# A macaron transformer block on one Trainium2 core: Winograd's seven block products in the global attention's value projection, and every local product on quarters of the array

## The chip, the cores and the metric

The kernel runs on one core of one Trainium2 chip; all data are fp32. The metric is device time in microseconds (us) of one execution; lower is better. Times of the kernel before are the median of three runs. Profiles are of one further execution each, with the granted TensorE clock beside the span (0.995 of full speed here).

## The reference

For 8 batches of 512 tokens with 256 channels, three stages follow one another:

```python
x = x + 0.5 * ffn(layernorm(x))        # two layers of local attention + GLU
x = x + global_attention(layernorm(x)) # 16 heads
x = x + 0.5 * ffn(layernorm(x))        # the same two layers, same weights

def global_attention(y, weight):
    heads = y.reshape(b, t, 16, 16).transpose(0, 2, 1, 3)
    attn = softmax(heads @ heads^T / 4)              # 512 x 512 for each head
    o = attn @ y                                     # every head averages whole rows of y
    return concat(o) @ weight                        # weight: (16*256, 256)

def local_attention(q, k, v):   # 8 heads of 64, windows of 128 tokens
    # a query sees its own window up to itself, and the window before from (i - 128) on
    return softmax(8 * q @ k^T + mask) @ v
```

Each ffn layer shifts half of the channels by a token, projects to q, k, v (`wqkv`), normalises and rotates q and k, runs the local attention, projects by `wo`, and then runs a GLU of width 682.

## The kernel before

**Who does what.** Two streams (`stream`, keys k = 0 and 1) run the ffn blocks, each for four batches, twice over; a third (`global_stream`) runs the global attention of a batch as soon as its first ffn is done. The three are interleaved step by step (each `yield` is a step). Nothing is issued directly: every operation is recorded with a rank, and `Plan.order` (line 270) then sets one static order for each engine by list scheduling, with a cost for each operation (`Plan.cost`, line 233), ring buffers for tiles, and a charge when TensorE changes the shape in which its array is used (`MODE`, line 183, names "whole", "columns", "halves", "quarters", "fours"). On the chip each engine's queue, SP's DMA queue too, runs in that order and waits at semaphores. All instructions carry the line of the planner's issuing loop (L369), so groups are told apart by tile names.

**TensorE.** An fp32 matmul appears as two MATMUL records, each with a weight load (LDWEIGHTS) of its own; counts below are of records. Tile names: `psum_bank` is any of the 8 PSUM banks.

**Global attention** (`global_heads`, line 956). For a batch: layernorm, then `zT`, the transposed activations as two tiles of 128 channels by 512 tokens (`work_gz`, lines 963 to 970). Since `attn @ y @ W_h = attn @ (y @ W_h)`, each head h first projects all tokens: y (512 x 256) times its block W_h (256 x 256). `front(h)` (line 975) loads W_h (`work_wa`, two buffers) and the head's 16 channels (`work_hT`, four small DMAs, two buffers) and gives three steps: `scores()` (line 987; four score tiles in four banks, Exp by ScalarE into `work_e`) and `project(0)`, `project(1)` (line 998). One `project` makes two token tiles of 128: four matmuls with 128 x 128 stationary operands from `zT` and 256 moving columns of W_h, then one VectorE copy of a whole bank into `work_xw`. So a head has 8 matmuls, 16 records. `attend(head, t)` (line 1017) multiplies: four matmuls of 256 columns, then one VectorE instruction that scales by 1/sum and adds to x. The loop at line 1031 runs the steps of head h+1 among the four `attend` of head h.

**Local attention** (`attention`, line 566). For each token tile t: `front(t)` (q, k, v), `scores(t)` (line 630), `values(t)` (line 732), `project(t)` (line 797, by `wo`). GpSimd (POOL) computes the rotary half `work_t`, the -0.5 power `small_rn` and the scaling of the probabilities. `far` is true for the middle six of each stream's eight blocks: there transposes go through DRAM and, for t > 0, both products run on 64 x 64 quarters of the array and leave out key halves that the mask removes. For the first tile (`nk == 1`), and for all tiles of the first and last block ("near"), scores use 64 rows by 128 columns ("halves", line 657) and values use 128 rows by 64 columns ("columns", lines 761 to 773), with one ScalarE copy `work_o<-psum_bank` after.

**GLU** (`glu`, line 819). The last 43 hidden rows of two token tiles are multiplied side by side in the two halves of the array (line 919).

**Weights.** `wo` of both layers stays resident (`load_attention`, line 393), GLU weights are loaded anew for each step by the second stream.

Of the kernel before, what the change touches and what calls it, by code (L numbers as in the profile page):

```python
# [11 lines left out]
ALU = mybir.AluOpType  # L12
# [164 lines left out]
class Plan:  # L177
# [55 lines left out]
    def cost(self, op):  # L233

        if op.engine == "tensor":

            lanes, op.mode = {}, "whole"
            for name, args, kw in op.calls:
                lane, t = 0, 109.0
                if name == "matmul":  # L240
                    a = kw["lhsT"]
                    lane, t = (a.region()[0], args[0].region()[0]), 2 * max(0.842 * elements(kw["rhs"]), 0.852 * a.shape[1])
                    k, m = a.shape
                    op.mode = "fours" if k <= 32 else "quarters" if k == m == 64 else "halves" if k <= 64 else "columns" if m <= 64 else "whole"
                lanes[lane] = lanes.get(lane, 0.0) + t
            busy = max(lanes.values())
            return busy, busy + 170
        name, args, kw = op.calls[0]
        n = max(elements(a) for a in (*args, *kw.values()) if hasattr(a, "shape"))
        if name == "dma_start":  # L250
            return 580.0, 2300.0
        if op.engine == "scalar":
            if name == "activation":
                op.mode = {AF.Exp: "exp", AF.Gelu: "gelu"}.get(args[2])
                busy = 70 + 0.82 * n + (105 if "bias" in kw else 0)
                return (busy + 93, busy + 310) if "accum_out" in kw else (busy, busy + 110)
            return 70 + 0.81 * n, 175 + 0.81 * n
        if op.engine == "vector":
            if name == "tensor_tensor_reduce":
                return 90.0 + n, 250.0 + n  # L260
            if name == "bn_stats":
                return 70.0 + n, 150.0 + n
            return 90 + 1.035 * n, 170 + 1.035 * n
        if name == "memset":
            return 80 + 0.85 * n, 100 + 0.85 * n
        if ALU.pow in args:
            return 350.0 + 157 * n, 400.0 + 157 * n
        return 210 + 1.98 * n, 250 + 1.98 * n
# [107 lines left out]
def macaron(ctx: ExitStack, tc: tile.TileContext, x, weight, wqkv, wo, w1, w2, b2, vecs, qk_scales, rotary, out):  # L376
# [16 lines left out]
    def load_attention(l):  # L393

        wq = wpool.tile([P, 2, 3 * INNER], F32, tag=f"wqkv{l}", name=f"wqkv{l}")
        for part in range(3):
            cols = slice(part * INNER, (part + 1) * INNER)
            nc.sync.dma_start(out=wq[:, :, cols], in_=wqkv[l, :, cols].rearrange("(k p) f -> p k f", p=P))
        o = wpool.tile([P, NPAIR, D], F32, tag=f"wo{l}", name=f"wo{l}")
        nc.sync.dma_start(out=o, in_=wo[l].rearrange("(k p) f -> p k f", p=P))  # L400
        return wq, o

    def load_glu(l):

# [18 lines left out]
    load_x(0)  # L423
    load_x(1)
    attention_weights = [load_attention(0)]
    glu_weights = [load_glu(0)]
    attention_weights.append(load_attention(1))
    tabs, vec = [], []
# [134 lines left out]
            later_of[k] = d.rearrange("p w -> (p w)").rearrange("(n f) -> n f", f=P)  # L563
        return later_of[k]

    def attention(k, y, l, far):
        wqkv_sb, wo_sb = attention_weights[l]
        z0 = zpool.tile([P, N + 1], F32, tag=f"z{k}", bufs=2)
        tiled = lambda t, c: y[:, t, c * P : (c + 1) * P]
        nc.scalar.copy(z0[:, :N], transposed(tiled, 0))  # L570
# [59 lines left out]
        def scores(t, pair, rn):  # L630
# [21 lines left out]
            for g in range(2):  # L652
# [1 line left out]
                quarters = far and nk == 2  # L654
                sps = [bank([P, 2, 3 * HALF if quarters else nk * P]) for _ in range(2)]

                pieces = [(slice(0, P), slice(0, nk * P), slice(0, nk * P))]
                if quarters:

                    pieces = []  # L660
# [71 lines left out]
        def values(t, probs):  # L732

            nk = min(t, 1) + 1
            o = work.tile([P, NPAIR, P], F32, tag="o", bufs=2)
            if far and nk == 2:

                pos = [bank([P, NPAIR, P]) for _ in range(2)]
                for g in range(2):
                    with plan.together():  # L740
                        for i in range(2):
                            for n in range(2):
                                for half in range(2):

                                    j = (1 - half, half)[n]
                                    q = slice(half * 2, half * 2 + 2) if n else slice(0, 4)
                                    rows = slice(half * HALF, (half + 1) * HALF)
                                    for par in range(2):
                                        h = 2 * i + par
                                        hd = 4 * g + h  # L750
                                        nc.tensor.matmul(
                                            pos[half][par * DH : (par + 1) * DH, 2 * g + i, q.start * 32 : q.stop * 32],
                                            lhsT=v[t - 1 + j][rows, hd * DH : (hd + 1) * DH],
                                            rhs=probs[g][rows, j, q, h, :],
                                            start=(n == 0),
                                            stop=(n == 1),
                                        )
                nc.scalar.copy(o, pos[0])
                nc.vector.tensor_add(o, pos[1], o)
                return o  # L760
            po = bank([P, NPAIR, P])

            def products(pair, turned):
                for j in range(nk):
                    for par in range(2):
                        hd = 2 * pair + par
                        nc.tensor.matmul(
                            po[par * DH : (par + 1) * DH, pair, :],
                            lhsT=v[t - (t + j) % 2][:, hd * DH : (hd + 1) * DH],
                            rhs=turned(par, j),  # L770
                            start=(j == 0),
                            stop=(j == nk - 1),
                        )

            if far:
                for g in range(2):
                    with plan.together():
                        for i in range(2):
                            products(2 * g + i, lambda par, j: probs[g][:, j, :, 2 * i + par, :])
            else:  # L780
                turned = []
                for n in range(NPAIR + 2):
# [7 lines left out]
                        turned.append(pT)  # L790
                    if n >= 2:
                        with plan.together():
                            products(n - 2, lambda par, j: turned[n - 2][:, par, j, :])
            nc.scalar.copy(o, po)
            return o

        def project(t, oT):
# [9 lines left out]
        for t in range(NT):  # L807
# [7 lines left out]
            o = values(t, probs)  # L815
            yield
        project(NT - 1, o)

    def glu(k, y, step, xb, far):
        l = step % DEPTH  # L820
# [90 lines left out]
        for t in (0, 2, 1, 3):  # L911
# [7 lines left out]
            with plan.together():  # L919
                for at, q in ((0, t - 2), (TAIL, t)):  # L920
                    rows = slice(at, at + LAST + 1)
                    nc.tensor.matmul(
                        pys[q],
                        lhsT=us[FULL][rows, q * P : (q + 1) * P],
                        rhs=w2_sb[rows, FULL, :],
                        start=False,
                        stop=True,
                    )
            for q in (t - 2, t):
                nc.vector.tensor_add(y[:, q, :], pys[q], y[:, q, :])  # L930
                if l == DEPTH - 1:
# [3 lines left out]
    def stream(k, blocks):  # L935

        for n, (b, second) in enumerate(blocks):
# [4 lines left out]
            for l in range(DEPTH):  # L942
                step = DEPTH * n + l
                far = FAR and 0 < n < len(blocks) - 1
                yield from attention(k, y, l, far)
                yield from glu(k, y, step, xs[b], far)

                if k == 1 and step + 1 < DEPTH * len(blocks):
# [7 lines left out]
    def global_heads(b):  # L956
# [13 lines left out]
            zT.append(z)  # L970

        def front(h):

            w = work.tile([P, 2, D], F32, tag="wa", bufs=2)
            nc.sync.dma_start(out=w, in_=weight[h * D : (h + 1) * D, :].rearrange("(c p) f -> p c f", p=P))

            hT = work.tile([P, N], F32, tag="hT", bufs=2)  # L980
            at = h % (P // AHD) * AHD
            for i in range(4):
                nc.sync.dma_start(out=hT[32 * i : 32 * i + AHD, :], in_=zT[h * AHD // P][at : at + AHD, :])
            rsum = gsmall.tile([P, NT], F32, tag="rsum")
            es, xw = [], []

            def scores():
                sps = [bank([P, N]) for s in range(NT)]
# [4 lines left out]
                for s in range(NT):  # L993
                    e = work.tile([P, N], F32, tag="e", bufs=2 * NT)
                    nc.scalar.activation(e, sps[s], AF.Exp, scale=1.0 / AHD**0.5, accum_out=rsum[:, s : s + 1])
                    es.append(e)

            def project(half):
                pv = bank([P, 2, D])
                with plan.together():  # L1000
                    for i in range(2):
                        s = 2 * half + i
                        for c in range(2):
                            nc.tensor.matmul(
                                pv[:, i, :],
                                lhsT=zT[c][:, s * P : (s + 1) * P],
                                rhs=w[:, c, :],
                                start=(c == 0),
                                stop=(c == 1),
                            )  # L1010
                xv = work.tile([P, 2, D], F32, tag="xw", bufs=4)
                nc.vector.tensor_copy(xv, pv)
                xw.append(xv)

            return es, xw, rsum, (scores, lambda: project(0), lambda: project(1))

        def attend(head, t):
            es, xw, rinv, _ = head
            pa = bank([P, D])
            with plan.together():  # L1020
                for s in range(NT):
                    nc.tensor.matmul(
                        pa, lhsT=es[s][:, t * P : (t + 1) * P], rhs=xw[s // 2][:, s % 2, :], start=(s == 0), stop=(s == NT - 1)
                    )
            xt = xs[b][:, t, :]
            nc.vector.scalar_tensor_tensor(xt, pa, rinv[:, t : t + 1], xt, ALU.mult, ALU.add)
# [122 lines left out]
```

## Time and profile before

| | |
|---|---|
| median of 3 runs | 3955.65 us (3954.25 to 3959.32) |
| profiled execution | 3959.6 us, its span 3957.8 us |
| TensorE clock granted | 0.995 |
| DMA | 400 MB, mean 101 GB/s; HBM 96 GB/s |
| projection `psum_bank<-work_wa,work_gz` | 2048 records of 256 columns, 477.4 us busy |
| attend `psum_bank<-work_xw,work_e` | 4096 records of 256 columns, 959.5 us busy |

How to read it: busy time is the union of an engine's instruction durations. A MATMUL record's duration contains its way through the array, so neighbours overlap: its mean ("384 ns") is not its price. The price in a stream is the distance from start to start, which a timeline gives: a merged entry `start, length, x16` is followed by the next entry's start. "Idle before" is the time that an engine stood still ahead of a group and what released it.

### The profile page before, as it was taken

The page shows a single profiled execution, that of the slowest core. Times are in us where ns is not written, and L with a number is a line of the kernel's source. Part 1 is how long each engine was busy: PE and PEld are TensorE (multiplying, and loading weights), DVE is VectorE, ACT ScalarE, POOL GpSimd, SP SyncE. Part 2 cuts the span into 40 slices and gives each one's busy share as a digit, 9 for nine tenths or more (in the row PEclk, how much of TensorE's full clock was granted, in tenths as well). Part 3 has the DMA queues.
Part 4 walks back from the last instruction along what each step waited for, and adds up shares of the span by engine and source line. Part 5 has one row for each costly group of instructions (what it writes and reads, how often), then busy time and mean ns, then how long its engine had stood idle before and what let it go on. Part 6 is the DMA issues. An engine that isn't in the chain of part 4 may idle for free.

```text
span 3957.8 us, 67863 instructions
## 1 busy us (share of the span) xinstructions
PE 3892.5 (98%) x23808; PEld 2675.0 (68%) x23808; DVE 2422.4 (61%) x6832; ACT 1779.5 (45%) x4556; POOL 1226.6 (31%) x1132
## 2 busy tenths in 40 slices
PE   8999999999999999999999999999999999999998
PEld 5565776766767667676676766767677666677665
DVE  7575655666566665665765667566556665526573
ACT  5564434535344353453544545354345353324462
POOL 6242323434133241331523424143223231103240
PEclk9999999999999999999999999999999999999999
DMA  3000543534435244352443534435325344110000
GB/s 116 1 23 28 153 137 103 154 98 138 124 119 148 87 142 119 118 153 86 138 142 101 156 93 143 137 102 161 96 90 154 93 132 128 57 37 5 1 23 11
DMA packets 437625, 400.43 MB, mean 101 GB/s; under 512 B 53954, under 2 KB 379172, under 8 KB 437284
## 3 DMA queue, kind: packets, MB, share of 16 engines
q1 hardware_dynamic: 436420, 394.76, 33.7%
q8 instruction: 189, 3.10, 0.3%
q10 hardware_dynamic: 864, 1.33, 0.1%
q14 instruction: 152, 1.25, 0.1%
HBM read 235.49 MB, written 143.66 MB: 96 GB/s over the span
## 4 chain that ended last, share of the span: by engine, by line
PE 55%; DVE 3%; ACT 2%; issue 2%; POOL 1%; DMA 0%; SPq 0%; POOLq 0%; DVEq 0%; ACTq 0%
PE psum_bank L369 55%; ACT work_p L369 1%; DVE work_p L369 1%; DVE work_qn L369 1%; POOL small_rn L369 0%; DVE small_ss L369 0%; POOL work_t L369 0%; SPq L369 0%; ACT work_qn L369 0%; DVE xpool_x L369 0%; DMA work_both<-dram_turned 0%; DMA work_p<-dram_turned 0%; ACT work_sq L369 0%; DVE work_both L369 0%; ACT work_both L369 0%
## 5 line engine op out<-in xcount | busy, mean ns | idle before, releaser
L369 PE MATMUL psum_bank<-work_xw,work_e 128*128 128x256 f32 x4096 | 959.5, 384 | 3.6 <-ACT work_e L369 2.5
L369 PEld LDWEIGHTS psum_bank<-work_xw,work_e 128*128 128x128 f32 x4096 | 762.6, 190 | 203.4 <-issue 42.3
L369 PE MATMUL psum_bank<-wpool_wqkv,zpool_z 128*128 128x512 f32 x1536 | 703.6, 597 | 1.3 <-ACT work_o L369 1.3
L369 ACT ACTIVATE work_p<-work_p,small_nmax,small_rn 128x192 f32<-128x192 f32 (+2 forms) x1024 | 543.8, 533 | 288.9 <-DVE small_nmax L369 187.0
L369 POOL TENSOR_TENSOR work_t<-work_qn,const_tab 128x256 f32<-128x256 f32 x512 | 388.7, 780 | 713.3 <-ACT work_qn L369 691.7
L369 PE MATMUL psum_bank<-zpool_z,wpool_w 128*128 128x512 f32 x1280 | 560.9, 597 | 1.5 <-DVE zpool_z L369 1.2
L369 POOL TENSOR_TENSOR work_p<-work_p,small_ri 128x768 f32<-128x768 f32 (+1 forms) x192 | 267.6, 1395 | 871.2 <-DVE small_ri L369 410.0
L369 POOL TENSOR_TENSOR small_rn<-small_ss,const_nhalf 128x8 f32<-128x8 f32 x256 | 486.7, 1902 | 137.8 <-DVE small_ss L369 130.9
L369 PE MATMUL psum_bank<-work_wa,work_gz 128*128 128x256 f32 x2048 | 477.4, 381 | 3.0 <-DVE work_gz L369 2.8
L369 ACT ACTIVATE work_e<-psum_bank 128x512 f32<-128x512 f32 x512 | 298.7, 596 | 396.6 <-PE psum_bank L369 390.1
L369 PEld LDWEIGHTS psum_bank<-wpool_wqkv,zpool_z 128*128 128x128 f32 x1536 | 284.4, 191 | 276.6 <-issue 261.6
L369 PEld LDWEIGHTS psum_bank<-zpool_z,wpool_w 128*128 128x128 f32 x1280 | 244.2, 192 | 302.2 <-issue 279.8
L369 PEld LDWEIGHTS psum_bank<-work_wa,work_gz 128*128 128x128 f32 x2048 | 384.9, 190 | 73.2 <-issue 14.9
L369 DVE SCALAR_TENSOR_TENSOR xpool_x<-psum_bank,gsmall_rinv,xpool_x 128x256 f32<-128x256 f32 x512 | 242.9, 476 | 275.0 <-PE psum_bank L369 272.2
L369 ACT COPY work_qn<-psum_bank 128x512 f32<-128x512 f32 x256 | 148.5, 583 | 374.8 <-PE psum_bank L369 322.9
L369 DVE TENSOR_REDUCE small_ss<-work_sq 128x8 f32<-128x512 f32 x256 | 172.5, 674 | 133.7 <-ACT work_sq L369 133.1
L369 DVE SCALAR_TENSOR_TENSOR work_p<-psum_bank,const_vec,work_p 128x512 f32<-128x512 f32 x128 | 95.8, 749 | 252.6 <-PE psum_bank L369 203.4
L369 PE MATMUL psum_bank<-wpool_wo,work_o 128*128 128x256 f32 x1024 | 246.7, 384 | 2.5 <-DVE work_o L369 1.6
L369 DVE COPY work_xw<-psum_bank 128x512 f32<-128x512 f32 x256 | 174.2, 681 | 121.8 <-PE psum_bank L369 120.5
L369 PE MATMUL psum_bank<-wpool_w,work_p 128*128 128x256 f32 x1024 | 242.7, 380 | 0.0
L369 DVE TENSOR_TENSOR ypool_y<-psum_bank,ypool_y 128x256 f32<-128x256 f32 x256 | 101.7, 419 | 216.2 <-PE psum_bank L369 213.2
L369 ACT COPY work_o<-psum_bank 128x512 f32<-128x512 f32 x128 | 74.7, 583 | 340.8 <-PE psum_bank L369 335.7
(89 smaller groups left out, 5025.8 us busy)
## 6 DMA issues: line engine op xcount, KB each, us to landing
work_p<-dram_quarters SPq DMA_DIRECT2D x576, 128.0 KB
dram_quarters<-work_p SPq DMA_DIRECT2D x288, 192.0 KB
dram_turned<-work_both SPq DMA_DIRECT2D x96, 512.0 KB
work_both<-dram_turned SPq DMA_DIRECT2D x384, 128.0 KB
work_wa<-in_weight_dram SPq DMA_DIRECT2D x128, 256.0 KB
wpool_w<-in_w_dram SPq DMA_DIRECT2D x48, 640.0 KB
work_hT<-work_gz SPq DMA_DIRECT2D x512, 32.0 KB
dram_turned<-work_p SPq DMA_DIRECT2D x48, 256.0 KB
```

The source lines that it names most:

```text
L369: getattr(getattr(nc, op.engine), name)(*map(real, args), **{k: real(a) for k, a in kw.items()})
```

## The change

**1. Projection by Winograd's form of Strassen.** y is cut in blocks of 256 tokens by 128 channels (`a11 a12 / a21 a22`), W_h in blocks of 128 x 128 (`b11 b12 / b21 b22`). Seven block products take the place of eight; each is two matmuls with 128 x 128 stationary operands and 128 moving columns: 14 matmuls, 28 records for each head. The sums of y are made once for each batch, those of W_h for each head, all on POOL; the sums of the products on VectorE, with one ScalarE copy.

```diff
+        sums = work.tile([P, 4, N // 2], F32, tag="sums")
+        for i, (u, v, op) in enumerate(
+            ((a21, a22, ALU.add), (sums[:, 0], a11, ALU.subtract), (a11, a21, ALU.subtract), (a12, sums[:, 1], ALU.subtract))
+        ):
+            nc.gpsimd.tensor_tensor(sums[:, i], u, v, op)
...
-            w = work.tile([P, 2, D], F32, tag="wa", bufs=2)
+            w = work.tile([P, 2, 4, P], F32, tag="wa", bufs=2)
+            nc.gpsimd.tensor_tensor(diffs[:, :2], blocks[:, 1::2], blocks[:, :2], ALU.subtract)
+            t1, t3, t2, t4 = (diffs[:, i] for i in range(4))
+            nc.gpsimd.tensor_tensor(t2, b22, t1, ALU.subtract)
+            nc.gpsimd.tensor_tensor(t4, b21, t2, ALU.subtract)
-            hT = work.tile([P, N], F32, tag="hT", bufs=2)
+            hT = work.tile([P, N], F32, tag="hT", bufs=1)
+            xw = work.tile([P, 4, 2, P], F32, tag="xw", bufs=2)
...
+            def product(*pairs):
+                ps = bank([P, len(pairs), 2, P])
+                with plan.together():
+                    for i, (left, right) in enumerate(pairs):
+                        for t in range(2):
+                            nc.tensor.matmul(ps[:, i, t, :], lhsT=left[:, t * P : (t + 1) * P], rhs=right, start=True, stop=True)
...
             def project(half):
-                xv = work.tile([P, 2, D], F32, tag="xw", bufs=4)
-                nc.vector.tensor_copy(xv, pv)
+                if half == 0:
+                    p1 = product((a11, b11))
+                    u1 = work.tile([P, N // 2], F32, tag="u1")
+                    nc.scalar.copy(u1, p1[:, 0])
+                    nc.vector.tensor_add(pairs[:, 0], product((a12, b21), (s2, t2)), spread(u1))
+                    return
+                ps = product((s3, t3), (s1, t1))
+                nc.vector.tensor_add(pairs[:, 1], ps, spread(whole[:, 2]))
+                nc.vector.tensor_add(whole[:, 2], ps[:, 1], whole[:, 1])
+                nc.vector.tensor_add(pairs[:, 1], product((a22, t4), (s4, b22)), pairs[:, 1])
```

`attend` reads the same 256 columns as two pieces of 128 (`rhs=xw[:, (slice(0, 4, 3), slice(1, 3))[s // 2], s % 2, :]`).

**2. Local products on quarters everywhere.** Scores of the first tile and of near blocks are cut into two halves of the queries. `values` has one form for all: key halves go to two banks `pos[0]`, `pos[1]`, the part that the mask removes is left out, and after the ScalarE copy VectorE adds the second bank (all queries, or the later half for `nk == 1`). The GLU's last matmul is cut in two halves of 64 tokens. The planner names every matmul of at most 64 x 64 "quarters".

```diff
-                pieces = [(slice(0, P), slice(0, nk * P), slice(0, nk * P))]
+                pieces = [(slice(q, q + HALF), slice(0, nk * P), slice(0, nk * P)) for q in (0, HALF)]
...
-            nc.scalar.copy(o, po)
+            nc.scalar.copy(o, pos[0])
+            q = slice(HALF if nk == 1 else 0, P)
+            nc.vector.tensor_add(o[:, :, q], pos[1][:, :, q], o[:, :, q])
...
+                    for half in (0, HALF):
                         nc.tensor.matmul(
-                            pys[q],
-                            lhsT=us[FULL][rows, q * P : (q + 1) * P],
+                            pys[q][half : half + HALF, :],
+                            lhsT=us[FULL][rows, q * P + half : q * P + half + HALF],
```

**3. `wo` in one buffer.** It is loaded for layer 0 at the start and then, by the second stream at the end of its attention, for the next step: 15 further loads of 512 KB.

```diff
+    def load_wo(l):
+        o = wpool.tile([P, NPAIR, D], F32, tag="wo")
...
+        if k == 1 and step + 1 < 2 * DEPTH * B // 2:
+            output_weights.append(load_wo((step + 1) % DEPTH))
```

## The prediction

> **What bounds the kernel now.** I read the page first: engines, clock.
>
> ```profile
> PE 3892.5 (98%) x23808; PEld 2675.0 (68%) x23808; DVE 2422.4 (61%) x6832; ACT 1779.5 (45%) x4556; POOL 1226.6 (31%) x1132
> PEclk9999999999999999999999999999999999999999
> ```
>
> TensorE is busy throughout at full clock. Busy time alone doesn't prove a bound, so next came the stretches, and what TensorE waited for in the long middle one, where the global attention lies.
>
> ```profile
> 0.00:400.00 400.00, 370.74 (x1948) 236.09 (x1949) 268.73 (x792) 223.89 (x528) 152.59 (x163) 0.99 0.14 43
> 400.00:3560.00 3160.00, 3147.49 (x19901) 2190.91 (x19900) 1920.72 (x5387) 1370.44 (x3581) 967.26 (x869) 1.00 0.41 120
> 3560.00:3958.00 398.00, 374.27 (x1961) 247.98 (x1960) 232.97 (x655) 185.20 (x449) 106.73 (x100) 0.98 0.03 10
> ...
> PE psum_bank L369 <- DVE work_gz L369: 2.8, 4, 1.2
> PE psum_bank L369 <- ACT work_e L369: 2.5, 3, 0.8
> PE psum_bank L369 <- DVE work_o L369: 1.6, 3, 1.0
> ```
>
> Columns of a stretch: its length, then busy time and count of PE, PEld, DVE, ACT, POOL. In 3160 us TensorE stands idle for 12.5, and its longest cause has 2.8. So in the middle a microsecond of TensorE work is a microsecond of time; only in the near blocks at both ends (29 and 24 us idle) do chains through other engines count.
>
> What remains is the price of TensorE work, start to start, from timelines: the projection, a stretch of 64x128 "halves", transposes.
>
> ```profile
> 2005.01 3.62 PE L369 MATMUL psum_bank<-work_wa,work_gz 128*128 128x256 f32 x16
> 2008.56 0.71 PE L369 MATMUL psum_bank<-work_hT 16*128 16x512 f32 x4
> ...
> 36.63 1.16 PE L369 MATMUL psum_bank<-work_kT,work_qT 64*128 64x128 f32 x16
> 37.73 0.70 PE L369 MATMUL psum_bank<-wpool_wqkv,zpool_z 128*128 128x512 f32 x1
> ...
> 3683.13 1.04 PE L369 MATMUL psum_bank<-const_ident,work_p 128*128 128x128 f32 x8
> 3684.00 1.04 PE L369 MATMUL psum_bank<-const_ident,work_qn 128*128 128x128 f32 x8
> ```
>
> A projection record of 256 columns: first to last start is 3.62 less one record's 0.38, over 15: 216 ns. A whole-array transpose, 128 columns and a fresh 128x128 operand: 0.87 us for 8, 109 ns.
>
> **Part 1, seven products: TensorE.** Before, a head takes 16 x 216 = 3.456 us; after, 28 records of 128 columns at a price that this trace does not show in that form. Each needs a full weight load, and the load's own row says 190 ns:
>
> ```profile
> L369 PEld LDWEIGHTS psum_bank<-work_wa,work_gz 128*128 128x128 f32 x2048 | 384.9, 190 | 73.2 <-issue 14.9 <-DVE work_gz L369 5.4 <-DVE xpool_x L369 0.7
> ...
> L369 DVE COPY work_xw<-psum_bank 128x512 f32<-128x512 f32 x256 | 174.2, 681 | 121.8 <-PE psum_bank L369 120.5
> L369 DVE TENSOR_TENSOR work_o<-psum_bank,work_o 128x512 f32<-128x512 f32 x72 | 49.1, 683 | 25.5 <-ACT work_o L369 23.4 <-PE psum_bank L369 2.0
> L369 DVE TENSOR_TENSOR ypool_y<-psum_bank,ypool_y 128x256 f32<-128x256 f32 x256 | 101.7, 419 | 216.2 <-PE psum_bank L369 213.2 <-ACT work_e L369 0.9 <-ACT work_p L369 0.9
> L369 POOL TENSOR_TENSOR work_t<-work_qn,const_tab 128x256 f32<-128x256 f32 x512 | 388.7, 780 | 713.3 <-ACT work_qn L369 691.7 <-issue 19.5 <-POOL work_t L369 1.2
> ...
> L369 ACT COPY work_both<-psum_bank 128x256 f32<-128x256 f32 x32 | 10.5, 374 | 12.5 <-PE psum_bank L369 12.4
> ```
>
> If loads followed one another end to end, 190 ns would be the price and the change a loss; the break-even is 3456 / 28 = 123 ns. Against that stands the halves stretch: its loads also take 188 ns and are of 128 columns for 128 moving ones, and yet single starts there are 36.847, 36.958, 37.070, 37.182: 112 ns. So most of the 190 is passage, and loads follow closer than they last. The transposes give 109 on the whole array, but their loads last only 140.
>
> Here the Trainium skill speaks against the change: "TensorE: Matmul & The Clock Gate", "Back-to-back issue gap", says that with a weight load for every matmul, 128 columns sustain about 81 ns, not the 56 of columns alone, a factor of 1.45. On 109 that estimates 158 ns: 28 x 158 = 4.42 us, +0.97 a head, +124 us. The halves row is fp32, with one load per matmul, and nearer; I keep it. Ends: 109 gives 3.052 us (-0.404 x 128 heads = -51.7 us), 112 gives 3.136 (-41.0 us). I take 109, as the shape is the whole array: **-52 us**. `attend` reads its columns in two pieces of 128; the far probabilities are read in pieces of 32 at full pace already: nothing.
>
> **Part 1, the other engines.** VectorE: two copies (2 x 681) become three sums of 512 at 683 and one of 256 at 419: 2468 - 1362 = +1.11 us a head, +142 us. ScalarE: 374 ns a head, +48 us. POOL: 780 for the double difference, and two of 128 columns at between 390 (half) and 780; I take 540: 1.86 us a head, +238, and 32 sums for eight batches, +25. VectorE goes to some 67% (with part 2), POOL to 38%, all beside TensorE: priced at nothing while TensorE's order has other ready work. If that cover is gone, the chain shows: the last product starts its sum only after 683 + 419 of earlier ones, and ends 683 later. While VectorE works that off, TensorE has the last product (8 x 109 = 0.87 us) and one `attend` (8 x 216 = 1.73 us): 2.6 against about 2.0 with signals. It fits, barely, with other VectorE work in between.
>
> New waits: POOL's differences wait for W_h's DMA; behind them stand the rotary products, powers and probability scalings, and behind those VectorE's `work_qn` and transposes. The DMA is issued about one head ahead (3958 / 128 = 31 us on average), and POOL is idle 69%. TensorE's second product waits for them, with everything behind it. VectorE's first sum waits for ScalarE's copy. Four banks instead of two are taken by a head, one at a time. `hT` with one buffer makes SP wait for the scores before; the next scores are a head away. By the trace each of these costs between 0 and, as an estimate, 0.25 us a head (a third of a VectorE sum): 0 to 32 us. I take 10, near the low end, because the present waits for `work_gz`, `work_e`, `work_xw` together come to 6 us in the middle.
>
> **Part 2, quarters.** Ideal times in columns at 0.843 ns (216 / 256):
> - Scores and the GLU's tail: twice the records, twice as many at once. Nothing.
> - Values, first tiles (512 "columns" records): the two key halves run on other quarters, in the longer one's time. Nothing.
> - Values, near blocks with two windows: 768 records, two at once, become 768 of 128 and 768 of 64 columns, four at once: 768 x 54 = 41.5 us to 768 x (27 + 13.5) = 31.1. **-10 us**.
>
> Changes of array shape: the halves stretch takes 37.73 - 36.63 = 1.10 us for 8 x 0.112 = 0.90, so 0.20 us for entry and exit, and the 512-column record behind it lasts 0.70 in place of 0.597. Scanning all MATMUL records in order I count 93 runs of halves and 108 of columns; 74 borders lie between two of halves, columns and quarters, and vanish when all are quarters. At 0.18 us each: **-13 us** (5 to 20, since the planner orders anew; below nothing is excluded as no border is added).
>
> VectorE's added sums: 24 x 0.683 + 32 x 0.419 = 30 us beside TensorE; in the near blocks up to 0.5 us each of chain, 16 us at most; part of my 10.
>
> **Part 3, `wo`.** 15 loads, 7.9 MB on 400: nothing in transfer. SP waits for the second stream's last projection, behind it all later DMAs; the first stream needs the tile some five steps later, of 3958 / 296 = 13.4 us. Hidden; a miss would cost a few us per layer.
>
> **Sum** against the profiled execution: 3959.6 - 52 - 10 - 13 + 10 = 3894.6. The median of the runs lies 3.95 below the profiled one: **3891 us**.
>
> **Rivals.**
> - *Loads bind (slower).* In the new product groups a whole-array load can't close up behind the one before as on halves. At 190 ns: 5.32 us a head, +239, with the rest of the sum 4182 us; at the skill's 158, 4066 us. It decides from 123 ns on. For it: the 190 ns row; against it: 112 and 109. 7%.
> - *Given back.* TensorE saves its 75 us, but product 2 waits for POOL's differences, or a bank or `attend` for VectorE's chain, 0.25 to 0.5 us a head: 32 to 64 us. At the middle of it, 3929 us. For it: four more dependent steps in each head; against it: POOL idle for 69%, VectorE for 39%, and 12.5 us of TensorE idle in 3160. 15%.
>
> **Numbers.** The forecast has 78%, its own range 3866 (109 ns, -20 for borders, nothing given back: 3874; and 8 of the 53 us idle in the near blocks gone with shorter groups) to 3917 (112 ns, -5 for borders, 17 given back). The range 3866 to 3932 reaches into the second rival. About 0.2% is what a measurement of this kernel tells from no change; slower takes the first rival and a sliver of the second, same a sliver of it: faster 0.88, same 0.04, slower 0.08.
>
> **What would show it.** Records `psum_bank<-work_wa,...` and `work_sums`: start to start 109 to 112 for 128 columns; 123 or more refutes the gain. TensorE's idle in the middle should stay below 30 us; waits for VectorE's `work_xw` or POOL's `work_wa` there above that mean the second rival. Runs of halves and columns: none. Near values in half as long groups. SP waiting longer than 60 us with the first stream's projection behind it would refute part 3.

## The result and the profile after

The changed kernel takes 3961.8 us (median of 22 runs, 3956.9 to 3970.9), the one before 3958.5 beside it (22 runs): ratio 1.0011 [1.0005, 1.0017]. Of the 65 us forecast nothing arrived. The two profiled executions can be compared as they stand: 3957.8 us before and 3955.6 after, both at a mean granted clock of 0.995, with TensorE at half clock for 41.8 us in each. Over all runs after, the mean is 0.994, beside 0.996 before; what that is worth stands with the experiments.

The engines' row of the page and the first two of the three stretches after (columns as before):

```profile
PE 3848.2 (97%) x27776; PEld 2688.1 (68%) x27776; DVE 2590.2 (65%) x7144; ACT 1852.8 (47%) x4710; POOL 1469.2 (37%) x1548
```

```profile
0.00:400.00 400.00, 367.54 (x2717) 229.36 (x2718) 282.80 (x809) 232.28 (x535) 160.12 (x174) 0.99 0.14 45
400.00:3560.00 3160.00, 3111.23 (x22360) 2215.22 (x22359) 2064.20 (x5660) 1412.11 (x3706) 1202.52 (x1271) 1.00 0.41 122
```

The middle stretch shows it: in the same 3160 us TensorE stands idle for 49 us where it was 12.5, and VectorE has 143 us more to do. What TensorE waits for there (total, times, longest; before, no line exceeded 2.8):

```profile
PE psum_bank L369 <- DVE work_xw L369: 15.6, 16, 2.6
PE psum_bank L369 <- DVE work_o L369: 11.7, 12, 2.9
PE psum_bank L369 <- POOL work_sums L369: 5.4, 6, 1.5
PE psum_bank L369 <- ACT work_e L369: 3.4, 4, 1.1
```

The first is the `attend` that waits for VectorE's last sum, the second the local projection that waits for VectorE's added second bank. One such place by the timeline, first TensorE, then POOL, then VectorE:

```profile
1117.62 0.61 PE L369 MATMUL psum_bank<-work_wa,work_gz 128*128 128x128 f32 x4
1118.07 0.61 PE L369 MATMUL psum_bank<-work_wa,work_sums 128*128 128x128 f32 x4
1118.61 1.14 PE L369 MATMUL psum_bank<-work_hT 16*128 16x512 f32 x8
1121.95 3.26 PE L369 MATMUL psum_bank<-work_xw,work_e 128*128 128x256 f32 x14 [2.21 <-DVE work_xw L369]
...
1115.18 1.79 POOL L369 TENSOR_TENSOR work_wa<-work_wa 128x256 f32<-128x256 f32 x3
...
1115.14 0.85 DVE L369 TENSOR_SCALAR work_p<-work_qn,small_mv,small_rstd 128x128 f32<-128x128 f32 x1
1116.45 0.61 DVE L369 TENSOR_SCALAR work_p<-work_qn,small_mv,small_rstd 128x128 f32<-128x128 f32 x1
1116.98 0.34 DVE L369 TENSOR_SCALAR work_p<-ypool_y,small_mv,small_rstd 128x128 f32<-128x128 f32 x1
1117.23 0.33 DVE L369 TENSOR_SCALAR work_p<-work_qn,small_mv,small_rstd 128x128 f32<-128x128 f32 x1
1117.49 0.70 DVE L369 STREAM_TRANSPOSE work_both<-work_qn 128x512 f32<-128x512 f32 x1
1118.12 1.20 DVE L369 STREAM_TRANSPOSE work_p<-work_p 128x1024 f32<-128x1024 f32 x1
1119.25 0.64 DVE L369 TENSOR_REDUCE small_ss<-work_sq 128x8 f32<-128x512 f32 x1
1119.81 0.67 DVE L369 TENSOR_TENSOR work_qn<-work_qn,const_tab 128x512 f32<-128x512 f32 x1
1120.41 0.16 DVE L369 TENSOR_SCALAR small_ss<-small_ss 128x8 f32<-128x8 f32 x1
1120.51 0.69 DVE L369 TENSOR_TENSOR work_qn<-work_qn,work_t 128x512 f32<-128x512 f32 x1
1121.12 0.68 DVE L369 TENSOR_TENSOR work_xw<-psum_bank,work_xw 128x512 f32<-128x512 f32 x1
```

Three readings. The pace: four product records of 128 columns from 1117.62 to 1118.07, 0.45 us, 112 ns each. The wait: the last product (the x4 at 1118.07) is through by 1118.7, but its sum starts at 1121.12, because VectorE's queue, hardly idle since 1114, holds the normalisation and rotation of a local tile ahead of it. TensorE has the eight score records to cover that, about 1.1 us, and then stands for 2.2. The slow queue: the same VectorE instruction (TENSOR_SCALAR, 128 x 128) takes 0.61 to 0.85 us while POOL forms differences of W_h (until 1116.97) and 0.33 to 0.34 after. Over the whole trace its median is 339 ns where no POOL instruction runs beside it (140 records) and 612 ns where the differences cover most of it (18 records).

Idle time alone does not show all of it, since a record's duration covers the start of a gap behind it. So I scanned all MATMUL records and split the span into columns at their measured pace, time lost where the array's shape changes, and what is left, called stalls (us); time lost at half clock is among the stalls:

| kernel | columns | changes of shape | stalls |
|---|---|---|---|
| before | 3693 | 170 | 86 |
| after | 3635 | 158 | 154 |
| difference | -58 | -12 | +68 |

So TensorE's work fell by 70, near the 75 forecast, and stalls took 68 of it back. Stalls over 0.25 us in the middle stretch number 61 after, 21 before. The split rests on a modelled pace; its sums lie 9 us under the span in both kernels.

A long wait can be paid twice. Two neighbouring stretches of 3.4 us after (columns as before, the granted clock behind POOL's):

```profile
1297.90:1301.30 3.40, 0.61 (x3) 0.59 (x4) 3.40 (x11) 0.00 (x0) 0.00 (x0) 1.00 0.37 101
1301.30:1304.70 3.40, 3.40 (x11) 2.30 (x13) 2.31 (x12) 2.23 (x8) 0.24 (x1) 0.50 0.48 171
```

TensorE waits for `work_o` in the first and then works through the second at half clock. In the middle stretch after, all four stretches at half clock come like this, right behind 3.4 us in which TensorE was busy for 0.6 to 1.5 only. In other runs some come without such a wait (one in e1 behind 0.15 us idle), so what sets one off is not shown here.

### The profile page after: what moved, and what is told of

The parts are those of the page before. It is cut to its first block, busy times and chain, and to the rows that moved or that the text cites. A ratio compares the mean times of both kernels' runs of the same rounds, so it can differ in the third digit from the quotient of the medians.

```text
span 3955.6 us, 77326 instructions
## 1 busy us (share of the span) xinstructions
PE 3848.2 (97%) x27776; PEld 2688.1 (68%) x27776; DVE 2590.2 (65%) x7144; ACT 1852.8 (47%) x4710; POOL 1469.2 (37%) x1548
## 4 chain that ended last, share of the span: by engine, by line
PE 71%; DVE 9%; ACT 4%; issue 3%; POOL 3%; DMA 1%; SPq 0%; DVEq 0%; POOLq 0%; ACTq 0%
PE psum_bank L369 71%; DVE work_p L369 3%; ACT work_p L369 3%; DVE work_qn L369 2%; POOL small_rn L369 1%; DVE small_ss L369 1%; POOL work_t L369 1%; DVE work_xw L369 1%; SPq L369 0%; DVE work_both L369 0%; DVE xpool_x L369 0%; DVE small_bnst L369 0%; DVE small_nmax L369 0%; DVE work_o L369 0%; ACT work_qn L369 0%
## 5 line engine op out<-in xcount | busy, mean ns | idle before, releaser
L369 PEld LDWEIGHTS psum_bank<-work_xw,work_e 128*128 128x128 f32 x4096 | 753.6, 190 | 214.6 <-issue 45.2
L369 POOL TENSOR_TENSOR work_wa<-work_wa 128x128 f32<-128x128 f32 (+1 forms) x384 | 223.1, 581 | 452.0 <-DMA work_wa<-in_weight_dram 386.1
L369 PE MATMUL psum_bank<-work_wa,work_sums 128*128 128x128 f32 x2048 | 293.8, 277 | 5.4 <-POOL work_sums L369 5.4
L369 PEld LDWEIGHTS psum_bank<-work_wa,work_sums 128*128 128x128 f32 x2048 | 266.6, 192 | 23.5 <-POOL work_sums L369 7.0
L369 DVE TENSOR_TENSOR work_xw<-psum_bank,work_xw 128x512 f32<-128x512 f32 (+1 forms) x384 | 228.0, 594 | 35.7 <-PE psum_bank L369 26.4
L369 PEld LDWEIGHTS psum_bank<-wpool_wo,work_o 128*128 128x128 f32 x1024 | 191.4, 192 | 68.0 <-DVE work_o L369 24.3
```

Source lines behind the costliest of these rows:

```text
L369: getattr(getattr(nc, op.engine), name)(*map(real, args), **{k: real(a) for k, a in kw.items()})
```

## Experiments

Theories. **A** (mine after the result): the products save what they should, and the wait for VectorE's work in each head returns it. **Rivals**: POOL's differences of W_h hold up the second product (P in the expectations); the single buffers of `hT` and `wo` hold up SP; the planner orders badly since it doesn't know the new costs (S); the new records themselves, or the static order at large, don't turn saved work into time. All times are medians, ratios are against the kernel before measured beside each run, and the clock is the mean of the runs' granted clocks (before: 0.996). e3, e4, e5, e9, e10, e13, e14 and e16 to e18 leave out part of the computation, so they are probes and not kernels to keep.

| run | us | ratio [95%] | clock |
|---|---|---|---|
| e1 part 1 alone | 3980.6 | 1.0061 [1.0048, 1.0073] | 0.992 |
| e2 part 2 alone | 3946.4 | 0.9972 [0.9961, 0.9982] | 0.996 |
| e3 no differences of W_h | 3965.7 | 1.0021 [1.0013, 1.0028] | 0.992 |
| e4 copies for sums | 3926.7 | 0.9924 [0.9911, 0.9936] | 0.996 |
| e5 before, 7 of 8 matmuls | 3915.2 | 0.9889 [0.9876, 0.9903] | 0.995 |
| e6 before, single buffers | 3956.0 | 0.9992 [0.9984, 1.0000] | 0.996 |
| e7 after, measured costs | 3962.7 | 1.0010 [1.0002, 1.0019] | 0.991 |
| e8 before, measured costs | 3979.7 | 1.0052 [1.0039, 1.0064] | 0.993 |
| e9 two banks | 3945.4 | 0.9968 [0.9955, 0.9980] | 0.994 |
| e10 e9, more VectorE work | 3961.3 | 1.0008 [0.9999, 1.0016] | 0.992 |
| e11 after, other order | 3973.4 | 1.0043 [1.0030, 1.0055] | 0.993 |
| e12 before, other order | 3966.9 | 1.0021 [1.0012, 1.0030] | 0.996 |
| e13 e9, no differences | 3951.0 | 0.9983 [0.9977, 0.9990] | 0.992 |
| e14 e9, other order | 3943.7 | 0.9963 [0.9951, 0.9976] | 0.993 |
| e15 e2, other order | 3946.0 | 0.9972 [0.9961, 0.9982] | 0.996 |
| e16 e4, other order | 3949.3 | 0.9975 [0.9965, 0.9985] | 0.995 |
| e17 before, 7 of 8, narrow | 3913.9 | 0.9890 [0.9876, 0.9905] | 0.997 |
| e18 e5, other order | 3917.9 | 0.9900 [0.9883, 0.9917] | 0.995 |

What the clock is worth can be estimated from runs of one kernel: in its 31 runs beside e16 the kernel before took 3951 to 3952 us where it was granted 0.998 and 3962 where it was granted 0.994, and a straight line through all of them falls by 2.8 us for each thousandth. A difference of two or three thousandths between two kernels is thus some 6 to 8 us, as an estimate. It may itself follow from the stalls, as above, so the times stand as measured, and differences of this size are not read.

### Each part alone

e1 keeps the products and one `wo`, with `scores`, `values` and the GLU's tail of before. e2 is the kernel before with those three as changed:

```diff
-                pieces = [(slice(0, P), slice(0, nk * P), slice(0, nk * P))]
+                pieces = [(slice(q, q + HALF), slice(0, nk * P), slice(0, nk * P)) for q in (0, HALF)]
...
+            nc.vector.tensor_add(o[:, :, q], pos[1][:, :, q], o[:, :, q])
```

> Part 1 and the single wo buffer, without the quarters. Medians so far: 3958 before, 3962 with the whole change, where TensorE's own work fell by about 75 us less 11 (112 ns in place of 109) and some 66 us came back as waits. Theory A (part 1 brings the waits: its VectorE chain and POOL's differences): saves 41 us, gives back about 60, so 3970 to 3980. Theory B (part 2's second bank and VectorE sums bring them): 3917 to 3930.

> Part 2 alone on the kernel before: quarters everywhere, eight products, wo resident. Its TensorE work falls by about 22 us (10 for masked parts, 12 for array shapes). Theory A (part 1 brings the waits): 3936 to 3945. Theory B (part 2 brings them): 3955 to 3990.

Part 1 alone (with the single buffers) costs 21 us, part 2 alone gains 13: the loss is in part 1. e2's middle stretch:

```profile
400.00:3560.00 3160.00, 3145.39 (x20939) 2191.99 (x20938) 1932.10 (x5423) 1326.22 (x3552) 979.39 (x874) 1.00 0.41 120
```

TensorE idles for 14.6 us there, about what it did before (12.5), though part 2's own sums are in it. The wait for `work_o` that stands second in the list after is thus hardly part 2's alone (3.2 us in e2, 11.7 after); it grows in the company of part 1.

### Does less TensorE work turn into time at all?

e5 leaves one matmul of eight out of the projection; e17 does the same and also cuts each of the rest into two of 128 columns, 28 records a head as in the change, all else as before:

```diff
-                        for c in range(2):
+                        for f, c in ((f, c) for f in range(2) for c in range(1 if s == 3 else 2)):
+                            cols = slice(f * P, (f + 1) * P)
...
-                                pv[:, i, :],
+                                pv[:, i, cols],
...
-                                rhs=w[:, c, :],
+                                rhs=w[:, c, cols],
```

> The kernel before, with one of a head's eight projection matmuls left out (the second half of the channels for the last token tile; this leaves out part of the computation): TensorE loses 2 x 216 ns x 128 heads = 55 us of work, and no other engine gets any. Theory V (the added work and hand-offs of VectorE and ScalarE ate the gain): nearly all comes through, 3903 to 3915. Theory C (TensorE was so near to the chains of the other engines that less TensorE work is worth only a part anyway): 3925 to 3950.

> The kernel before, with seven of a head's eight matmuls, each cut in two of 128 columns: 28 records of 128 columns a head as in the change, and nothing else of it (one matmul is left out, which leaves out part of the computation; no sums, no POOL work, eight-product layout and buffers). TensorE's work falls by 41 us at 112 ns. If the records deliver: 3920 to 3932. If narrow records cost something that their start-to-start distance doesn't show: 3945 to 3965.

e5 takes out 2 records x 216 ns x 128 heads = 55 us of work and gains 43. e17 takes out 128 x (3.456 - 28 x 0.112 = 0.320 us) = 41 us and gains 45. So the narrow records, weight loads included, deliver in full, and less TensorE work does turn into time. e17 has the changed kernel's count of product records, and its waits and products are these:

```profile
PE psum_bank L369 <- DVE work_o L369: 4.6, 5, 2.0
PE psum_bank L369 <- ACT work_e L369: 3.7, 5, 1.3
PE psum_bank L369 <- DVE work_xw L369: 3.6, 3, 1.5
```

```profile
L369 PE MATMUL psum_bank<-work_wa,work_gz 128*128 128x128 f32 x3584 | 434.9, 276 | 1.0 <-DVE work_gz L369 0.9
```

3584 is 2048 + 1536, the two product groups after; the wait for `work_xw` is 3.6, not 15.6. By the scan e17 has columns 3650, changes 171, stalls 84; e1 has 3650, 173 and 142. Same TensorE work, 58 us more stalls, and 67 us more time (61 between the profiled spans): that is the price of what surrounds the seven products. Part of it is clock: TensorE is at half clock for 52.7 us in e1's trace and for 31.3 in e17's, so up to half of the difference, 11 us. Each stands in one order only, but the difference is well beyond the 23 us that an order moved at most in the control below.

### POOL's differences

```diff
-            nc.gpsimd.tensor_tensor(diffs[:, :2], blocks[:, 1::2], blocks[:, :2], ALU.subtract)
-            t1, t3, t2, t4 = (diffs[:, i] for i in range(4))
-            nc.gpsimd.tensor_tensor(t2, b22, t1, ALU.subtract)
-            nc.gpsimd.tensor_tensor(t4, b21, t2, ALU.subtract)
+            t1, t3, t2, t4 = b11, b12, b21, b22
```

> The whole change, but POOL forms no differences of W_h: the blocks themselves are used in their place (this leaves out part of the computation), so TensorE's products wait for the DMA alone; the four sums for each batch stay. Theory P (POOL stands behind the DMA of W_h, with the local attention's POOL work behind it): 3962 - 40 to 50 = 3910 to 3925. Theory V (VectorE's longer chain and load): 3950 to 3962, at most 10 us better.

> The two-bank kernel (products added up on TensorE, two VectorE copies) also without POOL's differences of W_h: the blocks themselves are used (this leaves out part of the computation). Now no engine has more work than before and TensorE has 64 us less. If VectorE and POOL each suffice to eat the gain: 3900 to 3915, some 35 us below the 3945 of two banks with differences. If the products themselves or the order are the cause: 3935 to 3950.

e3 is 4 us slower than the whole change, e13 (e9 with this edit) 6 us slower than e9, in place of the 35 to 50 us faster that the rival asks for; both also ran at some two thousandths less clock, which by the estimate above can make up the 4 and 6. POOL's wait for W_h is long, but lies beside:

```profile
L369 POOL TENSOR_TENSOR work_wa<-work_wa 128x128 f32<-128x128 f32 (+1 forms) x384 | 223.1, 581 | 452.0 <-DMA work_wa<-in_weight_dram 386.1
L369 PE MATMUL psum_bank<-work_wa,work_sums 128*128 128x128 f32 x2048 | 293.8, 277 | 5.4 <-POOL work_sums L369 5.4
```

Behind 386 us of POOL standing at a DMA, TensorE's products wait 5.4 us, and those for the batch's sums (`work_sums`), not for the differences. That rival falls. So does, as a cause by itself, the slowing of VectorE beside these differences that the timeline showed: e3 and e13 are without them.

### Single buffers, and the planner's costs

e6 is before with one `hT` and one reloaded `wo`. e7 and e8 give the planner durations as measured (change of shape 190 ns for 150, a 128-column matmul 6 ns more, an Exp with a sum 105 ns more), in after and in before. The first edit is e6's, the second the core of the other two:

```diff
-            hT = work.tile([P, N], F32, tag="hT", bufs=2)
+            hT = work.tile([P, N], F32, tag="hT", bufs=1)
...
-    MODE = {"whole": 150.0, "columns": 150.0, "halves": 150.0, "quarters": 150.0, "fours": 290.0}
+    MODE = {"whole": 190.0, "columns": 190.0, "halves": 190.0, "quarters": 190.0, "fours": 290.0}
```

> The kernel before, with one buffer for hT and one for wo, reloaded for each layer; nothing else. If these waits of SP's queue give back part of the gain: 3968 to 3985. If they are hidden, as predicted: 3955 to 3962.

> The whole change, with four costs of the planner set to what the traces show: Exp with its sum 105 ns longer (its two records start 438 + 93 apart, 531 ns, where the planner takes 425 at 192 columns), a change of the array's shape 190 in place of 150, a matmul 6 ns longer at 128 columns. The work is the same, the order is made anew. Theory S (waits come back because the static order counts on ScalarE being done earlier than it is): 3915 to 3940. If the order is as good as the work allows: 3955 to 3970.

> The same costs in the kernel before. Theory S expects less here than in the whole change, since TensorE covers more: 3945 to 3958. If it gains as much as the whole change does, the costs are a matter of their own and do not explain what the change gave back.

SP's wait for TensorE over the whole span, before, after and in e6:

```profile
SPq L369 <- PE psum_bank L369: 1052.1, 318, 185.7
```

```profile
SPq L369 <- PE psum_bank L369: 1380.9, 354, 144.0
```

```profile
SPq L369 <- PE psum_bank L369: 1361.0, 336, 141.9
```

e6 reproduces the longer total wait of the DMA queue and no loss of time. e7 is where the changed kernel was. So neither rival, taken by itself, accounts for it. e8 is the surprise: the kernel before, nothing changed but the order in which it is issued, loses 21 us (some 8 of them by its lower clock, as an estimate). A difference of 10 to 20 us between two kernels here may be the order's.

ScalarE's table loads (1283 ns each, 108 before and 134 after) also change with the order, but don't go with the time: e1 has 96 of them and is slow, e16 has 144 and is faster than before.

### How much is the order? A control

e11, e12, e14, e15, e16 and e18 repeat six kernels with the planner's delay for a signal at 111 in place of 110 ns: nothing changes but the order.

```diff
-    SIGNAL = 110.0
+    SIGNAL = 111.0
```

> The whole change with one constant of the planner moved by a hundredth (a signal between engines 111 ns in place of 110): the same work in another static order. It shows how much the order alone moves the time. If little: within 5 us of 3962. If the order is a lottery: 10 us or more either way.

> The kernel before with the same constant at 111. If its order was a lucky one, it rises by 8 to 20 us, and part of what the change seems to give back is the loss of that order; if not, it stays within 5 us of 3958.

> Two banks with POOL's differences, planner's signal at 111: the same work in another order. If 3945 was an unlucky order: 3920 to 3935. If not: 3940 to 3957.

> Part 2 alone, signal at 111. The gain of part 2 (3946 at 110, 13 us) is real if it stays below the kernel before in the same order (3967): 3940 to 3957. If it was the order: 3960 to 3970.

> Copies for sums, signal at 111. Against the whole change in the same order (3973): if VectorE's sums cost some 35 us, 3930 to 3943; if the 3927 at 110 was a lucky order, 3945 to 3965.

> Seven of eight matmuls at 256 columns, planner's signal at 111 (one matmul left out). Against 3915 at 110 and the kernel before at 111, 3967: if less TensorE work comes through whatever the order, 3910 to 3930; if 3915 was a lucky order, 3935 to 3955.

The order moves before by 8 us, after by 12, copies by 23, and the others by 0.4 to 3. Means over both orders: before 3962.7, after 3967.6, part 2 alone 3946.2, copies 3938.0, two banks 3944.5, seven of eight 3916.6. Part 2's gain and the changed kernel's lack of one hold in both orders; e4's 3926.7 is partly luck.

### VectorE's sums

e4 keeps seven products, POOL's differences and ScalarE's copy of the first, but the other banks are copied out, not added: one by ScalarE, two by VectorE. e9 lets TensorE add the products up in two banks, with two VectorE copies as before and no ScalarE copy. e10 is e9 with three VectorE additions of 256 columns a head that nothing reads. The edits of e4, of e9, and of e10 on top of e9:

```diff
-                    nc.vector.tensor_add(pairs[:, 0], product((a12, b21), (s2, t2)), spread(u1))
+                    nc.vector.tensor_copy(pairs[:, 0], product((a12, b21), (s2, t2)))
...
-                nc.vector.tensor_add(pairs[:, 1], ps, spread(whole[:, 2]))
-                nc.vector.tensor_add(whole[:, 2], ps[:, 1], whole[:, 1])
-                nc.vector.tensor_add(pairs[:, 1], product((a22, t4), (s4, b22)), pairs[:, 1])
+                nc.scalar.copy(pairs[:, 1], ps)
+                nc.vector.tensor_copy(pairs[:, 1], product((a22, t4), (s4, b22)))
```

```diff
+                    nc.vector.tensor_copy(pairs[:, 0], product([[(a11, b11)], [(a12, b21), (s2, t2)]]))
...
+                nc.vector.tensor_copy(pairs[:, 1], product([[(s3, t3), (s1, t1)], [(a22, t4), (s4, b22)]]))
```

```diff
+                u1 = work.tile([P, N // 2], F32, tag="u1")
+                for _ in range(3):
+                    nc.vector.tensor_add(u1, a11, a12)
```

> The whole change, but the sums of the products are left out: the second and the last product are copied by VectorE as before (2 x 681 ns), the third bank by ScalarE; POOL's differences stay. This leaves out part of the computation. Theory V: 3962 - 40 to 50 = 3910 to 3925, and TensorE's waits for work_xw gone. Theory P: 3950 to 3962.

> The whole change, but the seven products are added up on TensorE into two banks (same 28 records a head, each with its load), which VectorE copies as in the kernel before; no sums of products, no ScalarE copy (this leaves out part of the computation). TensorE's work is that of the change, VectorE's and ScalarE's that of before, POOL's differences stay. Theory V (VectorE's and ScalarE's added work and hand-offs ate the gain): 3905 to 3920. If it stays above 3935, something else in part 1 costs (the records themselves, POOL, or the order).

> The same with three sums of 256 columns of SBUF data for each head on VectorE, some 1.0 us a head, about as much as the change adds, whose result nobody reads. If load on VectorE's queue is the cost: 25 to 40 us more than with two banks alone. If the hand-offs (four banks, a sum that waits for ScalarE, sums that TensorE waits for) are: within 10 us of it.

Without the sums the changed kernel gains 35 us (e4) or 16 (e9); over both orders 30 or 23. e10 gives VectorE more work back than e9 had lost: its busy time is 2476.0 us in e9, 2632.3 in e10 and 2590.2 after. Nobody waits for this work, and the time rises by 16 us. That lies between the two outcomes set out for e10 (within 10, or 25 to 40). It fits a cost of VectorE's load as such, a fuller queue in which whatever TensorE waits for comes later; but e10 stands in one order only, 16 us is within what an order moved e4 by, and some 8 of it can be the lower clock. That load alone costs is likely, not shown. What TensorE still waits for in e9, and the longest entry in e10:

```profile
PE psum_bank L369 <- DVE work_xw L369: 8.1, 9, 1.8
PE psum_bank L369 <- DVE xpool_x L369: 6.8, 3, 4.8
PE psum_bank L369 <- DVE work_gz L369: 6.5, 4, 4.1
PE psum_bank L369 <- POOL work_sums L369: 5.7, 6, 1.8
PE psum_bank L369 <- DVE work_o L369: 3.4, 5, 1.8
```

```profile
PE psum_bank L369 <- DVE work_o L369: 14.7, 12, 5.2
```

The sums are gone and the stalls are not (141 us by the scan), spread over several causes. Theory A holds for a share of the loss, 23 to 30 us, and not for all of it; how much of that share is VectorE's load and how much the handing over of the sums was not separated.

**What stays open.** Part 2 with seven products and nothing else should, as an estimate, stand near 3946 - 44 = 3902 us (e2 less the gain of e5 or e17). Two banks are at 3944.5. Some 42 us lie between them, in what e9 still has: POOL's differences (no, e13), single buffers (no by themselves, e6), the products' pace (no, e17), an order that happens to be bad (hardly, e14 agrees with e9 within 2 us), and three things not separated by a run: POOL's sums of each batch, ahead of a batch's first heads (direct waits of 5 to 6 us in e9, e13 and e14, and 6 to 13 for `work_gz` beside them); the layout of `work_xw` in one tile a head, where every `attend` needs both `project` steps and before the first two needed only `project(0)`; and these together with the longer wait in SP's queue. The second is read from the code and from the 8.1 us that `attend` still waits in e9; it was not isolated. At 0.994 and 0.993 beside 0.996, the clock may hold some 6 to 8 of the 42, as an estimate.

## Why the prediction was wrong, point by point

**"A microsecond of TensorE work is a microsecond of time"** held roughly for TensorE work alone: e5 returned 43 of 55, e17 45 of 41. "At full clock throughout" was read from slices that show 90% and more alike; TensorE was at half clock for 41.8 us.

**Seven products, -52 us.** The records run at 112 ns, the end that I did not take: -41. The rival that loads bind is refuted, by the timeline and by e17; so is the 158 ns estimated from the Trainium skill's rule ("TensorE: Matmul & The Clock Gate", "Back-to-back issue gap").

**Near values, -10, and borders, -13.** The first is about -17 (58 less 41, by the scan), the second -12: halves and columns are gone and the 74 borders with them, but the new order has ten others, so changes of shape fell from 922 to 858. Part 2 as a whole is -13 in one order and -21 in the other, against -10 - 13 plus some of the waits.

**`wo` and `hT`, nothing.** Right as far as e6 shows, which has these buffers without the products. SP waits up to 144 us, past the 60 that I had named as the sign of a loss, but it had waited up to 185.7 us before the change already: the sign was useless, and I could have seen that in the trace.

**The other engines, "priced at nothing while TensorE's order has other ready work", and waits +10.** This step failed. The added work was sized rightly: VectorE's outputs of the products went from 174 to 315 us, +141 against +142 forecast; ScalarE's copy takes 369 ns against 374, POOL's small differences 497 against 540:

```profile
L369 DVE TENSOR_TENSOR work_xw<-psum_bank,work_xw 128x512 f32<-128x512 f32 x256 | 174.7, 683 | 33.5 <-PE psum_bank L369 26.4 <-DVE work_xw L369 0.5
L369 DVE TENSOR_TENSOR work_xw<-psum_bank,work_u 128x512 f32<-128x512 f32 x128 | 87.2, 681 | 38.4 <-PE psum_bank L369 36.1 <-ACT work_u L369 1.6
L369 DVE TENSOR_TENSOR work_xw<-psum_bank,work_xw 128x256 f32<-128x256 f32 x128 | 53.3, 416 | 2.2
```

But stalls came to +68, where I had put +10 for waits, and TensorE's idle time in the middle to 49 us, past the 30 that I had named as the sign. I made three errors in it. I took the present waits (6 us in the middle) as a measure of future ones, though they belonged to an order with fewer dependent steps in it. I set the chain, 2.0 us, against a cover of 2.6 us as if VectorE took the sum at once; in the timeline shown it had 2.4 us of other work ahead of it, and the planner had put only 1.1 us of TensorE work behind the product. And I capped the waits at 0.25 us a head for the forecast, as an estimate from a third of one sum, when a whole sum and what stands ahead of it can be waited for. With the other terms (-41 for -52, -17 for -10, -12 for -13) the misses come to 63 us of the 68 between the forecast gain of 65 and the measured loss of 3; the lower mean clock of the runs after would fill most of the rest. Which of the added steps causes the larger part of these stalls stays open.

**The rival "given back"**, at 15%, is what happened in kind, though its top, some 3945 us, was also too low: 0.25 to 0.5 us a head was its size, and e1 against e17 puts it at 0.45 to 0.52 (58 to 67 us over 128 heads), with the products at -41 in place of -52. Of its mechanisms, VectorE's chain is shown for a part (e4, e9), POOL's differences are refuted (e3, e13). Its argument against itself, "VectorE [idle] for 39%", was the fallacy: idle time on average says nothing of when a queue in fixed order reaches the instruction that is waited for.

The version to keep is e2: quarters everywhere, eight products, both `wo` resident. It is faster than both kernels by little, 3946.4 us, 0.9972 [0.9961, 0.9982], and the same in another order (e15).

## What to carry to other kernels

In this static order, with one engine 98% busy, saved work on that engine turned into time (e5, e17), but the same saving with sums and hand-offs around it did not (e1). So price an exchange of TensorE work for additions elsewhere by the waits in the queue ahead of each new addition (what stands before it when its input is ready), not by the other engine's mean load; then try the saving alone (e17) and the addition alone (e10). And where an order is made by a planner, repeat each kernel in a slightly disturbed order, and look at the granted clock, before a difference of less than some 20 us in 4000 is called the change's.

## What the runs showed of the hardware

- A product record of 128 columns with a 128 x 128 load of its own takes 112 ns from start to start against 216 for 256 columns: halving the moving columns costs 3.7% (224 against 216), although each load's row lasts some 190 ns (190 before, 191 and 192 after).
- TensorE's clock falls to half for stretches of 3.4 us or a few times that, 41.8 us in all in the trace after; in the middle stretch after, each of the four followed 3.4 us in which TensorE was busy for 0.6 to 1.5.
- A VectorE instruction with 128 x 128 in and out of 339 ns takes 612 (medians) while POOL forms the differences of W_h beside it.
- POOL stood for 386 us at W_h's DMA, and SP for 1381 us at TensorE, with no time lost that a run could find.
- One planner constant moved from 110 to 111 ns, which changes only the order of issue, shifts the time of one and the same computation by 0.4 to 23 us.
